# A two-layer graph attention kernel: another order of work in its last stage

## The chip, the cores and the metric

The kernel runs on one core of a Trainium2 chip. The core has five engines that work through their own lists of instructions and wait for each other through semaphores: TensorE (PE, matrix products and transposes), VectorE (DVE, elementwise work and reductions), ScalarE (ACT, functions such as exp), GpSimd (POOL, here the issuer of the gathers) and SyncE (SP, here the issuer of plain transfers). Sixteen DMA engines move data between the large memory (HBM) and the core's own memory (SBUF). TensorE writes its products to a small memory, PSUM, from which VectorE and ScalarE read them.

The metric is the time of one execution on the device in microseconds (us). Before the change the median of three runs is 2330.81 us (2325.15 to 2334.34).

## What is computed

There are 4096 nodes with 512 features each and an adjacency matrix of 4096 by 4096, which is sparse (about 0.2% of its entries are set, many more for the first nodes than for the last). Layer 0 is a graph attention of eight heads; layer 1 is a graph attention of eight heads, a second attention of one head, and a small dense network. Both layers end with a residual sum and a normalisation. What the last stage of the kernel computes is the second half of layer 1:

```python
h2 = _gat_heads(x1, mask, Wo[None], ao[None])[0]     # one head, 512 wide
out = jax.nn.elu(h2)
out = jax.nn.relu(out @ lin1_w + lin1_b)             # 512 -> 1024
return out @ lin2_w + lin2_b                         # 1024 -> 512
...
x = _layernorm(x + _L1_gnn_ref(...), axis=-1)
```

Everything is in 32-bit floats.

## The kernel before, in words

Nodes are taken in 32 tiles of 128. The program first finds the edges of every tile (to about 500 us of the span), then runs the two attentions of eight heads, and then the last stage, from about 1400 us to the end at 2136 us. Only the last stage is changed. A dense path follows for inputs with too many edges, which is not taken with these inputs.

**Units.** The edges of a tile are held in chunks of 128. A unit (`Unit`) is up to six chunks of one tile; small tiles have one or two units, the first tile (the hub) many. For each unit the stage does this:

- `gather` (L1076): GpSimd issues an indirect DMA for each chunk. It fetches the 128 source rows of 514 floats from the table into a buffer `g`. There are four such buffers (`GT`), and a unit's gather is asked for four units ahead, when the sums of the unit that held the buffer have been issued.
- `spread` (L1101 to L1129), once for a tile, two tiles ahead: TensorE spreads the tile's own attention scores over its edges into `pss`; VectorE collects them later (`spread()`), into `s` and `ls`.
- `weights` (L1147 to L1158): three small VectorE steps give `z` from `s`, `ls` and the gathered scores, and ScalarE takes exp of it, giving `w`. It is called one unit ahead.
- `add` (L1187 and L1212): VectorE makes a selection matrix `sm` for each slot (a chunk and one half of the tile), weighted with `w`; TensorE multiplies the gathered rows with it and sums in `acc`. These are the *sums*.

When a tile's sums are complete: `inverse` (L1224) takes the reciprocal of the summed weights, `normal` (L1239) scales the sums to `o`, and `elu` (L1247 to L1249) takes two ScalarE steps to `ex` and returns a last VectorE step that makes the ELU in `o`. `turn` (L1456, L1457) lets TensorE transpose `o` (four transposes to `pt`) and ScalarE copy it to `sht`. There it waits until the tiles of a block (mostly four) are together.

**Pieces.** The dense network runs over blocks. Once the last tile of a block is turned, `ready` receives its pieces: as many of `first_dense` (each two of eight hidden groups, L1479, with bias and relu on ScalarE in L1482) as the block has tiles, and one of `second_dense` for each tile (L1491). A `second_dense` also loads the tile's residual row block `xr` (from `sx_d`, L1487, three buffers), adds the bias (L1488) and leaves a closing part in `open_`: adding the product (L1496), the normalisation on VectorE and ScalarE (L1253 to L1266) and the store (L1498). `close` carries that out; `piece` closes what is open and starts the next piece.

**What sets the order.** The schedule is written out by hand (`manual_schedule`): every engine gets its instructions in the order of the program's calls. A block's pieces are spread over the chunks of the next block: each chunk adds `pace` to `due`, and while `due` is at least 1 a piece is taken. In each step of the loop, before the change, the calls were: scores of a later tile, the turn of a tile that was finished in the step before, weights of the next unit, reciprocal for the tile just ended, this unit's sums, the gather, `close`, `normal` and the whole ELU (`fold`), collection of scores, and at the end the due pieces. After the loop come the last two turns and what is left of the pieces. PSUM holds two buffers for the products of the pieces (`p`), two for `acc`, one each for `pt` and `pss`; `sht` has two buffers and the hidden layer `shid` one.

Of the kernel before, what the change touches and what calls it, by code (L numbers as in the profile page):

```python
# [10 lines left out]
F32 = mybir.dt.float32  # L11
# [10 lines left out]
P = 128  # L22
N = 4096
F = 512
# [534 lines left out]
def sparse_path(  # L559
# [23 lines left out]
    nc = tc.nc  # L583
# [57 lines left out]
    x1_d = dram.tile([N, F], F32, name="sx1_d")  # L641
# [407 lines left out]
    def units_of(order):  # L1049
        units = []  # L1050
        for t in order:
            own = [
                Unit(t, [(p.first + i, n) for i, n in runs], slots)
                for p in pts if p.t == t for runs, *slots in p.units()
            ]
            own[0].first = own[-1].last = True
            units += own
        return units
# [186 lines left out]
    def elu(sb, o):  # L1245
        ex = sb.tile([P, F], F32, name="ex")
        nc.scalar.activation(ex, o, AF.Relu, scale=-1.0)  # L1247
        nc.scalar.activation(ex, ex, AF.Exp, scale=-1.0)  # L1248
        return lambda: nc.vector.scalar_tensor_tensor(o, ex, -1.0, o, op0=OP.add, op1=OP.max)  # L1249

    def layernorm(sb, y):
        bs = sb.tile([P, 6], F32, name="bs")
        nc.vector.bn_stats(bs, y)  # L1253
        mv = sb.tile([P, 2], F32, name="mv")
        nc.vector.bn_aggr(mv, bs)
        rs = sb.tile([P, 2], F32, name="rstd")
        lg, r = rs[:, 0:1], rs[:, 1:2]
        nc.scalar.activation(lg, mv[:, 1:2], AF.Ln, bias=eps)
        nc.scalar.activation(r, lg, AF.Exp, scale=-0.5)

        def rest():

            nc.vector.scalar_tensor_tensor(lg, mv[:, 1:2], EPS, r, op0=OP.add, op1=OP.mult)
            nc.vector.scalar_tensor_tensor(lg, lg, -0.5, r, op0=OP.mult, op1=OP.mult)
            nc.vector.scalar_tensor_tensor(r, lg, 1.5, r, op0=OP.add, op1=OP.mult)
            nc.vector.tensor_scalar(y, y, mv[:, 0:1], r, op0=OP.subtract, op1=OP.mult)  # L1266

        return rest
# [91 lines left out]
    with ExitStack() as pools:  # L1360
        big = pools.enter_context(tc.tile_pool(name="eb", bufs=1))
        sb = pools.enter_context(tc.tile_pool(name="es", bufs=2))
# [24 lines left out]
    sb = ctx.enter_context(tc.tile_pool(name="ls", bufs=2, reuse_waits="tile"))  # L1387
# [23 lines left out]
    with tc.tile_pool(name="tg", bufs=GT, side="right", reuse_waits="tile") as gp, \  # L1411
            tc.tile_pool(name="tb", bufs=1, side="right", reuse_waits="tile") as big, \
            tc.tile_pool(name="ta", bufs=2, space=PSUM, reuse_waits="tile") as pacc, \
            tc.tile_pool(name="tp", bufs=1, space=PSUM, reuse_waits="tile") as ps, tc.manual_schedule():

        few = NT - 12
        blocks = [[NT - 1, NT - 2], [NT - 3 - i for i in range(NJ)]]
        blocks += [[1 + b, few // 2 - b, few // 2 + 1 + b, few - b] for b in range(few // NJ)]  # L1420
        blocks.insert(3, [NT - 9, 0, NT - 8, NT - 7])
        blocks.append([NT - 10, NT - 11])
        assert sorted(sum(blocks, [])) == list(range(NT))
        order = [t for block in blocks for t in block]
        units = units_of(order)
        at = Attention(st2, gp, wk, pacc, ps)
        for _ in range(GT):
            nc.gpsimd.memset(gp.tile([P, GC, F + HS], F32, name="g"), 0.0)
        for u in units[:GT]:
            at.gather(u)  # L1430
        l1w = big.tile([P, FC, HID], F32, name="sl1w")
        nc.sync.dma_start(l1w, lin1_w.rearrange("(c p) o -> p c o", p=P))
        l2w = big.tile([P, HC, F], F32, name="sl2w")
        nc.sync.dma_start(l2w, lin2_w.rearrange("(c p) o -> p c o", p=P))
        l1b_r = big.tile([HC, P], F32, name="sl1b_r")
        nc.sync.dma_start(l1b_r, lin1_b.rearrange("(c p) -> c p", p=P))
        l2b = big.tile([P, F], F32, name="sl2b")
        nc.sync.dma_start(l2b, lin2_b.partition_broadcast(P))
        hts, hids, ready, open_ = {}, {}, [], []

        def fold(t):
            o = at.normal(sb, t)
            elu(sb, o)()
            return o

        def turn(t, o):
            b = next(b for b, block in enumerate(blocks) if t in block)
            j, nb = blocks[b].index(t), len(blocks[b])
            if j == 0:

                while any(r[1] == b - 2 and r[0] is first_dense for r in ready):
                    piece()
                hts[b] = big.tile([P, FC, NB], F32, name="sht", bufs=2)
            pt = ps.tile([P, FC, P], F32, name="pt")
            for c in range(FC):
                nc.tensor.transpose(pt[:, c, :], o[:, ts(c, P)], ident)  # L1456
            nc.scalar.copy(hts[b][:, :, ts(j, P)], pt)  # L1457
            if j == nb - 1:
                per = HC // nb
                ready.extend((first_dense, b, range(i * per, (i + 1) * per)) for i in range(nb))  # L1460
                ready.extend((second_dense, b, i) for i in range(nb))

        def piece():
            close()
            of, *what = ready.pop(0)
            of(*what)

        def close():
            while open_:
                open_.pop(0)()  # L1470

        def first_dense(b, ks):
            if 0 in ks:
                hids[b] = big.tile([P, HC, NB], F32, name="shid")
            for k in ks:
                n = len(blocks[b]) * P
                p1 = ps.tile([P, NB], F32, name="p1", tag="p", bufs=2)[:, :n]
                for c in range(FC):
                    nc.tensor.matmul(  # L1479
                        p1, l1w[:, c, ts(k, P)], hts[b][:, c, :n], start=(c == 0), stop=(c == FC - 1)  # L1480
                    )
                nc.scalar.activation(hids[b][:, k, :n], p1, AF.Relu, bias=l1b[:, k : k + 1])  # L1482

        def second_dense(b, j):
            t = blocks[b][j]
            xr = sb.tile([P, F], F32, name="xr", bufs=3)
            nc.sync.dma_start(xr, x1_d[ts(t, P), :])  # L1487
            nc.vector.tensor_add(xr, xr, l2b)  # L1488
            p2 = ps.tile([P, F], F32, name="p2", tag="p", bufs=2)
            for k in range(HC):  # L1490
                nc.tensor.matmul(  # L1491
                    p2, hids[b][:, k, ts(j, P)], l2w[:, k, :], start=(k == 0), stop=(k == HC - 1)
                )

            def rest():
                nc.vector.tensor_add(xr, p2, xr)  # L1496
                layernorm(sb, xr)()
                nc.sync.dma_start(out[ts(t, P), :], xr)  # L1498

            open_.append(rest)  # L1500

        for t in order[:2]:
            at.spread(t)()
        at.weights(units[0])
        l1b = big.tile([P, HC], F32, name="sl1b")
        pb = ps.tile([P, HC], F32, name="pt")
        nc.tensor.transpose(pb, l1b_r, ident[:HC, :HC])
        nc.vector.tensor_copy(l1b, pb)


        pace = {t: 0.0 for t in blocks[0]}
        for last, block in zip(blocks, blocks[1:]):
            chunks = sum(u.n for u in units if u.t in block)
            pace.update((t, 2 * len(last) / chunks) for t in block)
        due, folded = 0.0, None
        for i, u in enumerate(units):
            pos = order.index(u.t)
            spread = at.spread(order[pos + 2]) if u.first and pos + 2 < NT else None
            if folded:
                turn(*folded)  # L1520
                folded = None
            if i + 1 < len(units):
                at.weights(units[i + 1])
            if u.first and pos > 0:
                at.inverse(sb, order[pos - 1])
            at.add(u)
            if i + GT < len(units):
                at.gather(units[i + GT])
            close()
            if u.first and pos > 0:  # L1530
                folded = order[pos - 1], fold(order[pos - 1])
            if spread:
                spread()
            due = min(due + u.n * pace[u.t], 2.5)
            while due >= 1 and ready:
                due -= 1
                piece()
        if folded:
            turn(*folded)
        at.inverse(sb, order[-1])  # L1540
        turn(order[-1], fold(order[-1]))
        while ready:
            piece()
        close()
# [56 lines left out]
```

## Time and profile before

| What | Value |
|---|---|
| Median of the runs | 2330.81 us |
| The profiled execution, its own time | 2138.83 us |
| Its span, first to last instruction | 2136.3 us |
| TensorE busy, matrix products | 1721.8 us (81%) |
| VectorE, ScalarE, GpSimd busy | 1328.6, 663.4, 1162.0 us |
| Mean granted TensorE clock | 0.918 |
| First dense layer, L1479 | 228.9 us, 576 records |
| Second dense layer, L1491 | 226.7 us, 512 records |
| Sums of the last stage (L1212) from 1400 us on | 200.2 us, 1356 records |

The profile is of one execution, and all durations come from it. A 32-bit matrix product shows as two records. Start times of TensorE's records are measured while their ends are modelled, so a stretch that counts as busy can hold some waiting. "A <- B" in a list of waits means that A stood idle until B had finished. The clock is a share of TensorE's full speed.

### The profile page before, as it was taken

The page shows a single profiled execution, that of the slowest core. Times are in us where ns is not written, and L with a number is a line of the kernel's source. Part 1 is how long each engine was busy: PE and PEld are TensorE (multiplying, and loading weights), DVE is VectorE, ACT ScalarE, POOL GpSimd, SP SyncE. Part 2 cuts the span into 40 slices and gives each one's busy share as a digit, 9 for nine tenths or more (in the row PEclk, how much of TensorE's full clock was granted, in tenths as well). Part 3 has the DMA queues.
Part 4 walks back from the last instruction along what each step waited for, and adds up shares of the span by engine and source line. Part 5 has one row for each costly group of instructions (what it writes and reads, how often), then busy time and mean ns, then how long its engine had stood idle before and what let it go on. Part 6 is the DMA issues. An engine that isn't in the chain of part 4 may idle for free.

```text
span 2136.3 us, 29277 instructions
## 1 busy us (share of the span) xinstructions
PE 1721.8 (81%) x8987; PEld 1004.8 (47%) x8987; DVE 1328.6 (62%) x3920; ACT 663.4 (31%) x2311; POOL 1162.0 (54%) x1662
## 2 busy tenths in 40 slices
PE   4878777663798888857887888569999998998997
PEld 3655443221465565534555655344444444444444
DVE  5787777774889998837878878433434343433413
ACT  3346777664222232102333332111110212111121
POOL 5514444346777777727777777473547443543200
PEclk8999998786999999878999999889999999999999
DMA  6434566544777878727767776463546343534301
GB/s 229 132 109 168 188 250 238 201 153 130 228 233 231 248 242 243 208 67 191 196 185 195 195 198 190 151 165 102 156 119 177 113 128 96 148 103 120 96 19 46
DMA packets 132589, 351.94 MB, mean 165 GB/s; under 512 B 41922, under 2 KB 42954, under 8 KB 128454
## 3 DMA queue, kind: packets, MB, share of 16 engines
q0 software_dynamic: 74160, 206.25, 35.4%
q1 hardware_dynamic: 58262, 143.72, 19.1%
q8 instruction: 74, 1.21, 0.2%
q14 instruction: 93, 0.76, 0.1%
HBM read 347.31 MB, written 42.24 MB: 182 GB/s over the span
## 4 chain that ended last, share of the span: by engine, by line
PE 33%; DVE 17%; issue 16%; POOL 15%; DMA 12%; ACT 6%; SPq 0%; POOLq 0%; DVEq 0%; ACTq 0%
POOL g L1076 10%; DMA g<-table_t,idx 10%; PE acc L1212 10%; PE p L1479 9%; PE ph L697 6%; DVE g L1200 4%; PE p L1491 4%; DVE cand L884 2%; POOL s L944 1%; ACT sides L943 1%; DMA xr<-sx_d 1%; DVE cand L901 1%; DVE sm L1179 1%; DVE lst L899 1%; PE pl L967 1%
## 5 line engine op out<-in xcount | busy, mean ns | idle before, releaser
L1076 POOL DMA_INDIRECT g<-table_t,idx x927 | 937.8, 1012 | 535.9 <-issue 229.1
L1212 PE MATMUL acc<-g,sm 128*64 128x260 f32 (+2 forms) x4068 | 581.0, 416 | 182.7 <-DVE g L1200 141.6
L1212 PEld LDWEIGHTS acc<-g,sm 128*64 128x64 f32 x4068 | 327.9, 148 | 402.1 <-DVE g L1200 159.5
L697 PE MATMUL ph<-sw_t,xt 128*128 128x264 f32 (+1 forms) x1536 | 399.5, 409 | 54.3 <-ACT xt L686 47.8
L697 PEld LDWEIGHTS ph<-sw_t,xt 128*128 128x128 f32 x1536 | 296.5, 199 | 126.3 <-ACT xt L686 70.6
L1200 DVE TENSOR_TENSOR g<-g,wp 128x2048 f32<-128x2048 f32 (+3 forms) x132 | 348.9, 2644 | 3.4 <-ACT wp L1155 3.4
L884 DVE MAX8 cand<-key 128x8 f32<-128x353 f32 (+55 forms) x467 | 196.3, 446 | 77.6 <-PE key L878 76.8
L1479 PE MATMUL p<-sht,sl1w 128*128 128x512 f32 (+1 forms) x576 | 228.9, 553 | 0.5 <-DVE xr L1496 0.5
L1491 PE MATMUL p<-sl2w,shid 128*128 128x512 f32 x512 | 226.7, 597 | 0.0
L686 ACT ACTIVATE xt<-pt 128x128 f32<-128x128 f32 x384 | 101.1, 278 | 214.3 <-PE pt L683 213.9
L1479 PEld LDWEIGHTS p<-sht,sl1w 128*128 128x128 f32 x576 | 108.0, 191 | 111.6 <-issue 106.0
L1491 PEld LDWEIGHTS p<-sl2w,shid 128*128 128x128 f32 x512 | 95.2, 190 | 119.8 <-issue 119.4
L1147 DVE TENSOR_TENSOR z<-s,g 128x16 f32<-128x16 f32 (+8 forms) x291 | 46.6, 175 | 162.7 <-DMA g<-table_t,idx 161.6
L877 PE MATMUL key<-sg,s_identb 128*128 128x512 bf16 (+1 forms) x258 | 111.5, 433 | 14.3 <-DVE cand L884 9.0
L1482 ACT ACTIVATE shid<-p,sl1b 128x512 f32<-128x512 f32 (+1 forms) x72 | 46.0, 639 | 242.8 <-PE p L1479 242.8
L1249 DVE SCALAR_TENSOR_TENSOR o<-ex,o 128x512 f32<-128x512 f32 x64 | 44.2, 691 | 122.0 <-ACT ex L1248 121.8
L848 ACT ACTIVATE sg<-raw 128x4096 bf16<-128x4096 int32 (+1 forms) x39 | 116.9, 2998 | 6.3 <-DMA raw<-in_adj_dram 3.4
L710 ACT COPY hrow<-ph 128x260 f32<-128x260 f32 (+2 forms) x194 | 70.5, 372 | 152.3 <-PE ph L697 152.0
L878 PE MATMUL key<-frac,places 128*128 128x512 bf16 (+1 forms) x258 | 111.4, 433 | 2.7 <-POOL places L784 2.7
L1187 DVE TENSOR_SCALAR sm<-iota_n,nl,w 128x64 f32<-128x64 f32 x339 | 83.6, 327 | 31.2 <-ACT w L1158 31.2
L1155 ACT ACTIVATE wp<-z 128x32 f32<-128x32 f32 (+3 forms) x132 | 27.2, 206 | 211.2 <-DVE g L1200 211.2
L1496 DVE TENSOR_TENSOR xr<-p,xr 128x512 f32<-128x512 f32 x32 | 22.0, 689 | 93.6 <-PE p L1491 93.2
(185 smaller groups left out, 1853.5 us busy)
## 6 DMA issues: line engine op xcount, KB each, us to landing
raw<-in_adj_dram SPq DMA_DIRECT2D x31, 2048.0 KB, 7.7
table_t<-hrow SPq DMA_DIRECT2D x64, 260.0 KB, 3.2
xr<-in_x_dram SPq DMA_DIRECT2D x64, 256.0 KB, 3.9
g<-table_t,idx POOLq DMA_INDIRECT x927, 3.8
table_t<-hrow SPq DMA_DIRECT2D x32, 257.0 KB, 4.4
sx_d<-o SPq DMA_DIRECT2D x32, 256.0 KB, 4.0
xr<-sx_d SPq DMA_DIRECT2D x32, 256.0 KB, 4.4
out_dram<-xr SPq DMA_DIRECT2D x32, 256.0 KB, 2.3
```

The lines of the kernel that those rows point to most:

```text
L686: nc.scalar.activation(xt[:, c, :], pt[:, c, :], AF.Copy, accum_out=st.xparts[:, c, t : t + 1])
L697: nc.tensor.matmul(ph[:n], columns(c), st.w[:, c, j], start=(c == 0), stop=(c == FC - 1))
L848: nc.scalar.activation(sg[:, ts(i, w)], raw[:, ts(i, w)], AF.Sign)
L877: nc.tensor.matmul(out_, ident_b, sg[:, j:e], start=True, stop=False)
L878: nc.tensor.matmul(out_, places[:, w], frac[:, j - w * KW : e - w * KW], start=False, stop=True)
L884: nc.vector.max(out=cand[:, at : at + 8], in_=part)
L1076: nc.gpsimd.indirect_dma_start(out=u.g[:, k, : self.st.row], out_offset=None, in_=self.st.table[:, :], in_offset=bass.IndirectOffsetOnAxis ...
L1187: nc.vector.tensor_scalar(sm[:, at + i], of_g, node[k], u.w[:, k], op0=OP.is_equal, op1=OP.mult)
L1200: nc.vector.tensor_mul(body, body, wp[:, :, :, None].to_broadcast(body.shape))
L1212: nc.tensor.matmul(out_[g * HN : (g + 1) * HN], sm[:, slot], rows(k), start=start, stop=stop)
L1479: nc.tensor.matmul(p1, l1w[:, c, ts(k, P)], hts[b][:, c, :n], start=(c == 0), stop=(c == FC - 1))
L1491: nc.tensor.matmul(p2, hids[b][:, k, ts(j, P)], l2w[:, k, :], start=(k == 0), stop=(k == HC - 1))
```

## The change

It reorders the calls of the last stage's loop, and takes the load of the residual rows out of `second_dense`. In each step the calls now are: scores of a later tile, one due piece if there is one, this unit's sums, the gather, collection of scores, then for a tile that has just ended the reciprocal, `normal` and the two ScalarE steps of the ELU, then the weights of the next unit, the last VectorE step of the ELU, `close`, the turn of a tile finished in an earlier step, and further due pieces. So on ScalarE the exp of the weights stands behind the ELU's two steps, and the turn's copy behind the exp. `due` is added to at the start of a step and no longer at its end. `piece` also loads the residual rows of the next piece if that is a `second_dense`.

```diff
-        hts, hids, ready, open_ = {}, {}, [], []
-
-        def fold(t):
-            o = at.normal(sb, t)
-            elu(sb, o)()
-            return o
+        hts, hids, resid, ready, open_ = {}, {}, {}, [], []
...
             of, *what = ready.pop(0)
+
+            if ready and ready[0][0] is second_dense:
+                rows_of(*ready[0][1:])
             of(*what)
+
+        def rows_of(b, j):
+            t = blocks[b][j]
+            if t not in resid:
+                resid[t] = sb.tile([P, F], F32, name="xr", bufs=3)
+                nc.sync.dma_start(resid[t], x1_d[ts(t, P), :])
...
-            xr = sb.tile([P, F], F32, name="xr", bufs=3)
-            nc.sync.dma_start(xr, x1_d[ts(t, P), :])
+            rows_of(b, j)
+            xr = resid.pop(t)
...
-        due, folded = 0.0, None
+        due, folded = 0.0, []
         for i, u in enumerate(units):
             pos = order.index(u.t)
             spread = at.spread(order[pos + 2]) if u.first and pos + 2 < NT else None
-            if folded:
-                turn(*folded)
-                folded = None
-            if i + 1 < len(units):
-                at.weights(units[i + 1])
-            if u.first and pos > 0:
-                at.inverse(sb, order[pos - 1])
+            due = min(due + u.n * pace[u.t], 2.5)
+            if due >= 1 and ready:
+                due -= 1
+                piece()
             at.add(u)
             if i + GT < len(units):
                 at.gather(units[i + GT])
-            close()
-            if u.first and pos > 0:
-                folded = order[pos - 1], fold(order[pos - 1])
             if spread:
                 spread()
-            due = min(due + u.n * pace[u.t], 2.5)
+            last, rest = units[i - 1].t if u.first and i else None, None
+            if last is not None:
+                at.inverse(sb, last)
+                o = at.normal(sb, last)
+                rest = elu(sb, o)
+            if i + 1 < len(units):
+                at.weights(units[i + 1])
+            if rest:
+                rest()
+            close()
+            if folded:
+                turn(*folded.pop(0))
+            if rest:
+                folded.append((last, o))
             while due >= 1 and ready:
                 due -= 1
                 piece()
-        if folded:
-            turn(*folded)
-        at.inverse(sb, order[-1])
-        turn(order[-1], fold(order[-1]))
+        last = order[-1]
+        at.inverse(sb, last)
+        o = at.normal(sb, last)
+        elu(sb, o)()
+        for what in folded + [(last, o)]:
+            turn(*what)
```

## The prediction

> **What bounds the kernel now.** I read the granted clock first, then the page, the windows by time, the waits of the last stage, and last the timeline around one long wait. The page says TensorE (PE) is the busiest engine, and the change touches the last stage alone. That stage starts about 1400 us into the span and gives PE nearly all the work of the last 690 us.
>
> ```profile
> PE   4878777663798888857887888569999998998997
> PEclk8999998786999999878999999889999999999999
> ```
>
> Row one is PE's busy share in tenths, row two its granted clock. From slice 28 on PE stands at 8 to 9 tenths. A gain can only come from the idle tenth or from the slow clock. I therefore cut the stage where the blocks of dense work begin (the first `first_dense` matmul of each block).
>
> ```profile
> core 0: us, PE busy (x), PEclk, DMA share, GB/s
> 1449.61:1478.30 28.69, 23.56 (x97) 0.94 0.36 109
> 1478.30:1570.48 92.18, 88.73 (x402) 0.96 0.44 125
> 1570.48:1682.35 111.87, 105.26 (x460) 0.97 0.55 158
> 1682.35:1776.98 94.63, 83.84 (x326) 0.93 0.39 114
> 1776.98:1863.64 86.66, 81.36 (x335) 0.98 0.40 115
> 1863.64:1953.54 89.90, 83.78 (x350) 0.98 0.45 128
> 1953.54:2036.03 82.49, 79.89 (x333) 1.00 0.28 84
> 2036.03:2125.25 89.22, 85.94 (x233) 0.98 0.10 30
> ```
>
> Columns: stretch, its length, PE's busy time (count), clock, DMA. Busy time hides some loss, because a matmul that waits inside a group or runs at a low clock counts as busy. So I price PE's work by undisturbed groups of the timeline: a piece (8 wide products, 16 records) takes 6.97 us from start to start, sums 2.75 us for 24 records, a turn 0.55, a score group about 0.2. Length minus work, per row: 8.1, 9.9, 19.5, 17.3, 8.8, 10.7, 4.6, 4.3. **Lost in all: 83 us.**
>
> ```profile
> PE pt L1456 <- DVE o L1249: 29.1, 8, 4.3
> PE acc L1212 <- DVE sm L1187: 12.0, 14, 2.3
> DVE xr L1488 <- DMA xr<-sx_d: 68.3, 21, 5.5
> DVE z L1147 <- DMA g<-table_t,idx: 23.6, 11, 3.6
> ```
>
> These are waits in us, times, longest. Turns wait for the ELU's last step 8 times; sums wait for their selection matrices `sm` 14 times. VectorE (DVE) itself waits 68 us for the residual rows, which are loaded only when needed.
>
> ```profile
> 1845.88 7.13 PE L1491 MATMUL p<-sl2w,shid 128*128 128x512 f32 x16
> 1853.06 1.96 PE L1212 MATMUL acc<-g,sm 128*64 128x257 f32 x16
> 1859.27 1.11 PE L1456 MATMUL pt<-s_ident,o 128*128 128x128 f32 x4 [4.26 <-DVE o L1249]
> 1860.40 3.31 PE L1212 MATMUL acc<-g,sm 128*64 128x257 f32 x16
> 1863.64 7.13 PE L1479 MATMUL p<-sht,sl1w 128*128 128x512 f32 x16
> ```
>
> One block boundary. The piece at 1845.88 is the block's last, so for a while PE has only sums and turns. It idles 4.26 us; then the turn takes 1.11 instead of 0.60 and the sums 3.31 instead of 1.96.
>
> **What the Trainium skill says.** "TensorE: Matmul & The Clock Gate", Part 1, has the array fall to half rate after an idle window of about 3.4 us and recover after as much work. The trace agrees: after gaps of 3.65 to 4.26 us turns last about 1.1 us, while after gaps of 2.60 and 2.73 they last 0.66. So a gap kept under 3.4 us saves a further 1.5 to 3 us. The same page, Part 1 under engine queue depths, calls ScalarE (ACT) and VectorE strict first-in first-out. The trace agrees: at 2051.11 an ELU whose input was ready at 2037.1 starts only after the last bias-and-relu of a piece. Hence program order is what must be followed here. "DMA: Bandwidth & Descriptors" (Anatomy of one DMA) fits a transfer from GpSimd's queue as 2.0 us plus its bytes at 436 GB/s, by estimate 2.6 us for a gather of 128 rows of 514 floats; the trace has 3.7 us from issue to landing, and that is used.
>
> **The change, part by part.** Write S and F for a piece of the second and first dense layer, A for a unit's sums, T for a turn, | for a tile's scores. Instruction counts are unchanged on PE, DVE, ACT, and so are POOL's gathers in number and order; only places change. TensorE's program order over the sixth row's cycle:
> before: F A F | A F T A F | A S T A S | A S T A S | A T A F F
> after: F F A | F A F A T | S A S A T | S A S A T | A A T F F
>
> 1. *Turn one unit later, behind that unit's sums.* Its input is then an ELU from the step before, done while PE summed. The 29.1 us go, except 2.7 at 2053.20 (below), and with them the half clock.
> 2. *Due piece ahead of the sums.* 7 us of PE work cover a unit's `sm`, so the sm waits in the steady part go: 1.0 to 1.4 us each at 1535.9, 1765.1, 1843.6, 1930.2, 1941.1, plus about 0.4 inside each.
> 3. *Residual rows loaded one piece ahead.* SP's queue then has the next load ahead of the previous store (two loads, then store and load in turn), so a load no longer waits for a normalisation. Three buffers hold: one normalised, one used, one landing. DVE's 68 us disappear; PE gains what part 2 counts, plus the tail.
> 4. *Weights before the ELU's last step on DVE, but ACT's exp for them behind the ELU's two ACTIVATEs; the copy behind both.* This costs. Per first unit w comes 1.3 us later (2 x 0.63). Queued behind the ELU's last step on DVE are the normalisation and the next unit's sm, for which PE waits where no piece is due. Also T and F are now adjacent where a block begins: PE waits for the copy, 0.58 plus hand-overs, about 0.9 us.
>
> *Worked boundary, after:* S ends at 0. DVE's closing chain (add 0.69, statistics 0.7 + 0.2, ACT's two 0.5, three of 0.16, scaling 0.55, as at 1853.06 to 1856.5) ends at 3.5. PE: A to 1.9, T to 2.5, scores to 2.75; the next A waits for its first sm at 3.85 (1.1 lost) and ends at 5.9. DVE: sm to 4.6, scores 5.0, reciprocal 0.17, normal 0.74 to 5.9; ACT: ELU 7.2, w 7.4; DVE: last ELU step 7.95, sm 8.3. The third A waits 2.4 us and ends at 10.3, T at 10.9, F starts at 11.9. Lost: 1.1 + 2.4 + 0.9, with edges 4.75 us. No gap reaches 3.4 us. With 12-matmul sums (24 records in place of 16) the waits shrink and it loses 3 to 3.7.
>
> *The sum*, lost after against before by row: 3 for 8.1; 8 for 9.9 (the hub tile's scores in four cuts, 1539 to 1549, stay); 9 for 19.5 (6 is the hub's gather limit: POOL issues a chunk each 1.30 us there without a break); 6.5 for 17.3; 4.75 for 8.8; 4 for 10.7; 4 for 4.6; 2 for 4.3. The last: the wait at 2053.20 stays, since the final ELU is still behind the relus. But the load at 2122.25 no longer holds the last addition (2126.79, though its matmuls ended at 2125.3: 1.5 us), and about 0.8 goes at 2099. Saved: 83 - 41 = 42 us. From this I take off 5, an estimate for gathers: four units' buffers, four to six chunks of 1.30 us plus 3.7 us landing each, are waited for 23.6 us on DVE now under cover, and a quicker PE uncovers some. **37 us.** The profiled execution (2138.83 us) would then take 2102. The runs' median, 2330.81, is 192 us longer, and no view shows where; I carry the difference over unscaled, for a gap made of DVE and ACT latencies has no reason to shrink there: **2294 us**.
>
> Unknown costs: the copy's wait, 0 (the piece's weights already loaded) to 2.5 us (behind a late w), nine times, 0 to 22 us, taken 8. The uncovered gathers, 0 to 15 us, taken 5. The half clock, if the 1.1 and 2.4 us gaps fall in one window, 0 to 2 us at seven boundaries, taken 0.
>
> **Rivals.** *B, the wait only moves:* sums at a boundary wait for the ELU chain as turns did. For it: a third A and both queues in order. Against: the worked chain. At 8 instead of 4.75 us at seven boundaries, 23 us are given back, 14 remain: 2317. *C, slower:* the copy is last in ACT's step, behind w, and w's z waits for a gather. Where a block begins, F needs that copy, so a late gather now stops PE for 7 us (a gather wait as the longest, 3.6, the copy 0.9, and then half clock, 2.5) at eight block starts: 56 - 42 = +14, 2345. It decides from 5.3 us per block start. For it: gathers land barely in time near the hub. Against: at a boundary the needed gather was issued two sums and a piece earlier, some 13 us, and takes 9 to 12. *D, no change:* the runs' extra 192 us are slower gathers, and the stage is bound by them, not by PE's order: 2331. For it: the unexplained difference. Against: nothing in the profile.
>
> **How the numbers follow.** Forecast 0.66 (own range 2272 to 2312), B 0.12, C 0.14, D 0.08. 0.5% is 11.7 us, about what a measurement of this kernel can tell. Faster: 0.66 and half of B, 0.72; same: half of B and D, 0.14; slower: C, 0.14. The range, 2268 to 2326, takes the unknown costs at their ends and B.
>
> **What would show it.** Right: PE's waits on `o` nearly gone, DVE's wait on `xr` near zero, turns of 0.6 us, the clock 1.0 in the 0.93 rows, new waits of sums on `sm` of 1 to 2.4 us at boundaries, about seven. Wrong: gaps above 3.4 us before the first F of a block, or gather waits on DVE above 40 us; then C or B. If the profiled time falls by 37 and the median doesn't, D.

## The result, and the profile after

| | median, us | runs |
|---|---|---|
| before | 2334.49 (2321.84 to 2350.53) | 20 |
| after | 2333.68 (2322.99 to 2344.67) | 20 |

The ratio is 1.0004, with a 95% interval of 0.9987 to 1.0021: no difference, where 37 us less were forecast.

One thing has to be known to read the numbers: the time went with the chip. On one chip the kernel before took 2133 to 2139 us in all its runs, on three others 2321 to 2353 us. They are called the *2135 chip* and the *2335 chips* below. The profile of before shown above has the time of the first sort. The runs to be predicted, and the profile of after, have that of the second.

First the page of after: PE's busy share and clock, and the head of the chain that ended last.

```profile
PE   4777776645676787764667787856979998989998
PEclk9889997766878899886888899877989999999999
PE 52%; DVE 14%; issue 11%; another core or an unknown queue 8%; ACT 6%; POOL 6%; DMA 2%; SPq 0%; POOLq 0%; DVEq 0%; ACTq 0%
```

8% of the chain is put down to a releaser that the profile doesn't know. The page of before has no such entry. The waits of the last stage of after (us, times, longest; "remote" is again the unknown releaser):

```profile
DVE s L1117 <- remote: 36.8, 5, 13.4
ACT sht L1452 <- remote: 17.6, 3, 5.9
PE acc L1212 <- DVE sm L1187: 13.1, 13, 3.6
PE pss L1101 <- DVE s L1117: 10.6, 3, 5.6
PE p L1483 <- ACT sht L1452: 10.4, 4, 4.7
DVE xr L1492 <- DMA xr<-sx_d: 3.2, 1, 3.2
PE pt L1451 <- DVE o L1249: 2.3, 1, 2.3
```

What the change aimed at has happened: the turns' wait for the ELU fell from 29.1 to 2.3 us, VectorE's wait for the residual rows from 68.3 to 3.2. In their place stand waits of the first dense layer for the turn's copy (L1452) and of the scores for their collection (L1117), and both consumers wait for something "remote". Here is such a block start in the timeline (start, length, engine, line, operation, count, idle time before and its releaser):

```profile
1959.44 0.21 ACT L1158 ACTIVATE w<-z 128x6 f32<-128x6 f32 x1 [2.04 <-DVE z L1147]
...
1960.52 1.00 POOL L1076 DMA_INDIRECT g<-table_t,idx  x1 [0.30 <-issue]
...
1960.84 0.66 PE L1451 MATMUL pt<-s_ident,o 128*128 128x128 f32 x4
...
1961.82 1.00 POOL L1076 DMA_INDIRECT g<-table_t,idx  x1 [0.30 <-issue]
...
1963.12 0.99 POOL L1076 DMA_INDIRECT g<-table_t,idx  x1 [0.30 <-issue]
1965.55 0.58 ACT L1452 COPY sht<-pt 128x512 f32<-128x512 f32 x1 [5.90 <-remote]
1965.73 1.00 POOL L1076 DMA_INDIRECT g<-table_t,idx  x1 [1.62 <-remote]
...
1966.19 3.78 PE L1483 MATMUL p<-sht,sl1w 128*128 128x512 f32 x4 [4.70 <-ACT sht L1452]
```

The transposes end at 1961.50. ScalarE has been free since 1959.65. Yet the copy starts at 1965.55, 4.05 us late, while GpSimd issues a gather each 1.30 us; GpSimd then also waits 1.62 us for the unknown. TensorE has nothing else to do and stands for 4.70 us. Afterwards its wide products run 0.85 us apart in place of 0.43. The Trainium skill ("TensorE: Matmul & The Clock Gate", Part 1) has the array at half rate after an idle window of about 3.4 us; the trace agrees here as it did before.

The same happens at two other block starts (3.71 us late at 1871.44, 4.27 at 2050.93) and in the hub tile's scores (1725.4 to 1731.1, where PE waits 5.63, 2.49 and 2.46 us for a collection). At the other four block starts of this stretch the copy is 0.04 to 0.33 us late. Gathers go on around three of these too, but there GpSimd had issued only one, three or four of them since its last pause when the transposes ended; ahead of the three late copies it had issued at least five without a pause. That is a pattern of seven starts and no tested rule.

To compare kernels I use the **dense part**: from the first full-width record of `first_dense` to the end of the last `second_dense`, the prediction's rows two to eight. It is 647.0 us in the profile of before and 652.5 in that of after.

### The profile page after: what moved, and what is told of

The parts are those of the page before. It is cut to its first block, busy times and chain, and to the rows that moved or that the text cites. A ratio compares the mean times of both kernels' runs of the same rounds, so it can differ in the third digit from the quotient of the medians.

```text
span 2320.7 us, 29242 instructions
## 1 busy us (share of the span) xinstructions
PE 1752.6 (76%) x8987; PEld 1020.7 (44%) x8987; DVE 1332.4 (57%) x3920; ACT 661.1 (28%) x2311; POOL 1165.3 (50%) x1662
## 4 chain that ended last, share of the span: by engine, by line
PE 52%; DVE 14%; issue 11%; another core or an unknown queue 8%; ACT 6%; POOL 6%; DMA 2%; SPq 0%; POOLq 0%; DVEq 0%; ACTq 0%
PE acc L1212 15%; PE ph L697 13%; PE p L1483 10%; PE p L1495 9%; DVE g L1200 3%; DVE cand L884 2%; POOL g L1076 2%; PE pt L683 1%; POOL s L944 1%; ACT sides L943 1%; DVE cand L901 1%; DVE lst L899 1%; DMA g<-table_t,idx 1%; PE pl L967 1%
## 5 line engine op out<-in xcount | busy, mean ns | idle before, releaser
L1212 PE MATMUL acc<-g,sm 128*64 128x260 f32 (+2 forms) x4068 | 565.1, 403 | 192.4 <-DVE g L1200 90.3
L697 PE MATMUL ph<-sw_t,xt 128*128 128x264 f32 (+1 forms) x1536 | 432.1, 434 | 139.1 <-ACT xt L686 96.3
L1212 PEld LDWEIGHTS acc<-g,sm 128*64 128x64 f32 x4068 | 316.7, 142 | 426.6 <-issue 147.1
L697 PEld LDWEIGHTS ph<-sw_t,xt 128*128 128x128 f32 x1536 | 319.5, 215 | 220.3 <-ACT xt L686 114.9
L1117 DVE TENSOR_REDUCE s<-pss 128x64 f32<-128x192 f32 (+20 forms) x108 | 32.3, 299 | 123.4 <-remote 80.6
```

The lines of the kernel that those rows point to most:

```text
L697: nc.tensor.matmul(ph[:n], columns(c), st.w[:, c, j], start=(c == 0), stop=(c == FC - 1))
L1212: nc.tensor.matmul(out_[g * HN : (g + 1) * HN], sm[:, slot], rows(k), start=start, stop=stop)
```

## The experiments

The theory at the start was that the moves did save what was worked out, and that something not in the profile of before takes it back. Its rivals were that the reordering never saved anything, or that a part of it costs (weights behind the ELU, copy behind the weights).

**Both kernels again, unedited.**

> The kernel before, unchanged, profiled once more, to compare like with like. 'Dense part' means the time from the first 512-wide product of the first dense layer to the end of the last product of the second: 647.0 us in the first profile of before (1478.3 to 2125.3), 652.5 us in the profile of after (1658.8 to 2311.3). Theory 1 (the profiled execution was a rare one): a normal execution has a span near 2330, in which waits for TensorE's results end 2 to 7 us after the matmul, most of them in the two attention stages; the dense part of before is then longer than 647, about 655 to 690 us, and the change gains little or nothing because its own order is hit as much. Theory 2 (the reasons of the prediction were wrong in themselves): the dense part of before is 645 to 650 us also in a normal execution, and the reordering simply moved its waits.

> The kernel after, unchanged, profiled once more. If its execution is of the short kind (span near 2100 to 2140), theory 1 expects a dense part of about 605 to 620 us, as the prediction worked it out (647 less 37), and theory 2 expects 645 to 652. If it is of the long kind (span near 2320), both expect about 652, with copies to sht that start 3 to 5 us after their transposes at three or more block starts.

On one 2335 chip (before there: 2333.38) they took 2332.8 and 2326.86 us, and their dense parts were 649.0 and 655.0. The dense part of before starts at 1670.29 there and at 1478.30 in its first profile: the 192 us lie ahead of it, and it is itself only 2 us longer. Most of the waits for "remote" that before has on this chip (whole program) lie in that stretch, and the first profile has none anywhere:

```profile
ACT xt L686 <- remote: 123.0, 14, 17.2
ACT hrow L710 <- remote: 82.6, 22, 7.7
POOL g L1076 <- remote: 44.4, 23, 4.0
```

After, run again, has four late copies (2.63 to 5.65 us, one of them just ahead of the dense part), and at the hub's scores TensorE waits 4.25, 3.87 and 2.47 us for collections. So the late results are no accident of one execution.

**Parts of the change, on 2335 chips.** Early load alone, in the kernel before:

```diff
             close()
             of, *what = ready.pop(0)
+            if ready and ready[0][0] is second_dense:
+                rows_of(*ready[0][1:])
...
-            xr = sb.tile([P, F], F32, name="xr", bufs=3)
-            nc.sync.dma_start(xr, x1_d[ts(t, P), :])
+            rows_of(b, j)
+            xr = resid.pop(t)
```

> The kernel before with only the load of the residual rows one piece ahead. The prediction put the waits behind late residual rows at about 5 x 1.5 us in the steady part and 2.3 us at the end: theory 1 and the prediction expect 5 to 12 us less than before (0.2 to 0.5%), theory 2 expects no difference (within 3 us).

The kernel after with the turn ahead of the sums, so that sums lie between a turn and the first dense layer:

```diff
+            if folded:
+                turn(*folded.pop(0))
             at.add(u)
...
             close()
-            if folded:
-                turn(*folded.pop(0))
```

> The kernel after with one edit: the turn of an older tile is issued ahead of the unit's sums in place of behind them, so that where a block's first piece starts, a unit's sums lie between the transposes and the matmuls that need their copy. Theory 1 (late copies at block starts are what gave the gain back: 4.4, 4.7 and 4.9 us of waiting at three starts, each followed by some 2 us at half clock) expects 15 to 30 us less than after. Theory 2 (the waits move to wherever the chain on VectorE ends) expects within 5 us of after.

That order again with the next unit's `weights` called ahead of `inverse`, `normal` and the ELU:

> As the version with the turn ahead of the sums, and with the next unit's weights ahead of the reciprocal, the norm and the ELU of the tile just ended, so that their exp stands ahead of the ELU's two steps on ScalarE. By the worked boundary the next sm is 1.3 us (two ELU steps) earlier at some nine places without a due piece: 5 to 12 us less than the version it is made from, if the chain over ScalarE bounds there; no difference (within 4 us) if late signals from TensorE do. A gather that is late now holds the norm as well, which could cost up to 5 us.

The kernel after without the early load (the three lines in `piece` taken out):

> The kernel after without the early load of the residual rows: the reordering alone. The early load alone made before 20.8 us faster. If the two parts add up, this is 15 to 25 us slower than before (ratio 1.006 to 1.011); if the reordering only took away what the early load could still give (both fill the same holes), it is within 5 us of before.

| kernel | us | runs | ratio to before, 95% interval | dense part |
|---|---|---|---|---|
| early load alone | 2312.6 | 6 | 0.9904 (0.9874 to 0.9933) | 639.8 |
| turn ahead of the sums | 2318.02 | 7 | 0.9931 (0.9900 to 0.9963) | 637.7 |
| and weights first | 2335.91 (before there 2344.59) | 22 | 0.9960 (0.9948 to 0.9973) | 645.9 |
| after without early load | 2374.47 (before there 2344.59) | 5 | 1.0138 (1.0114 to 1.0162) | 670.5 |

On these chips the early load is worth 1% alone, and the other moves of the change cost what it brings. It saved more than the 5 to 12 us expected; the profiled execution, the slowest of the six, has 9.2 us in its dense part, and the rest wasn't traced. Where the sums lie behind the turn, TensorE goes on working, and the copy has only to be done by their end: in the dense part one copy is 2.41 us late, no wide product waits for a copy, and the part is 17 us shorter than that of after on the same chip. Putting the weights first doesn't help further. The reordering without the early load cost 30 us, more than the 15 to 25 expected.

**Is it the gathers?** In the last stage of both kernels the gather is replaced by plain loads of as many rows of the table on SyncE's queue. These fetch wrong rows, so the gather is left out; all other work stays.

```diff
             for k, c in enumerate(u.chunks):
+                if self.st.heads == 1:
+                    nc.sync.dma_start(u.g[:, k, : self.st.row], self.st.table[ts(c % NT, P), :])
+                    continue
                 nc.gpsimd.indirect_dma_start(
```

> The kernel before, whose last stage loads each chunk with a plain DMA of 128 table rows from SyncE in place of GpSimd's indirect gather: the bytes move, GpSimd issues nothing, the rows are not the right ones. Theory G (while GpSimd issues gathers back to back, a result of TensorE that nothing follows on TensorE is signalled only when that run of issues ends): before has few such results in its dense part, so it stays near 649 us less the hub's gather limit, 632 to 645. Theory P (a result is late whenever TensorE pauses, whoever else works): no change beyond the hub, the same 632 to 645.

> The kernel after with the same plain loads. Theory G: the copies to sht start within 0.3 us of their transposes at all block starts (3.7 to 4.3 us late at three of them in after), the collections of the hub's scores likewise (2.3 to 5.4 us late), and the dense part is 605 to 622 us, against 652 to 655 with gathers: at least 15 us below the plain version of before. Theory P: the copies stay 3 to 6 us late at three or more block starts and the dense part is within 8 us of the plain version of before.

Each ran once. Before became slower (2369.69 against 2344.59), missed its forecast and tells nothing of gathers: its residual loads now stand behind the plain loads on SyncE, and VectorE waits 184.5 us for them. After fell to 2291.61 us on the same chip, and its dense part to 619.0. Its waits have no "remote" left in the last stage, and the first dense layer waits 0.7 us at most for a copy:

```profile
PE p L1486 <- ACT sht L1455: 5.4, 8, 0.7
PE pt L1454 <- DVE o L1252: 2.3, 1, 2.3
PE pss L1104 <- DVE s L1120: 1.2, 4, 0.3
```

So with no gathers from GpSimd the late results are gone from the change's order. (How much the order itself saves can't be read from this, because the plain version of before gives no base.) What it is about a gather was left: its issue, a GpSimd that is merely busy, or the wait for the rows. Two more kernels load as the last one does and give GpSimd something useless to do for each load, either a gather into a buffer that nothing reads, or a fill of about the same length (0.84 us against 1.00):

```diff
                     nc.sync.dma_start(u.g[:, k, : self.st.row], self.st.table[ts(c % NT, P), :])
+                    spare = self.gp.tile([P, P], F32, name="spare", bufs=4)
+                    nc.gpsimd.indirect_dma_start(
+                        out=spare,
+                        out_offset=None,
+                        in_=x1_d.rearrange("n (q w) -> (n q) w", w=P),
+                        in_offset=bass.IndirectOffsetOnAxis(ap=idx[:, c : c + 1], axis=0),
...
                     continue
```

```diff
                     nc.sync.dma_start(u.g[:, k, : self.st.row], self.st.table[ts(c % NT, P), :])
+                    spare = self.gp.tile([P, 896], F32, name="spare", bufs=1)
+                    nc.gpsimd.memset(spare, 0.0)
                     continue
```

> The plain-load version of after, and beside each plain load GpSimd issues one indirect gather of 128 rows of 512 bytes into a spare buffer that nobody reads (the output is that of the plain version). These gathers wait for nothing but their own buffers, so GpSimd issues all 309 back to back, some 400 us of issuing, until about 1980 to 2050 of the span, and is silent afterwards. Theory G (back-to-back issuing of gathers on GpSimd holds back TensorE's signals) expects copies to sht 2 us or more late at most block starts while the issuing lasts, none after it, and a dense part 15 us or more above the 619.0 us of the plain version. Theory D (a late signal needs GpSimd itself to wait for TensorE, or the gathered rows to be used) expects copies within 0.3 us throughout and a dense part of 617 to 625.

> The same with a memset of 128 x 896 floats on GpSimd in place of each idle gather (0.78 us each by the 2.70 us that 3120 columns take), so GpSimd is as busy but issues no DMA. If it is the issuing of DMAs that matters, copies stay within 0.3 us and the dense part at 617 to 625; if any busy GpSimd holds signals back, copies are late as with gathers in the first half of the stage and the dense part is 630 or more.

These ran on the 2135 chip (before there 2135.2): 2106.93 and 2112.56 us, no late copy in either. A second pair ran there too, with 2108.41 and 2107.81 us and dense parts of 618.3 and 620.7:

> The changed kernel with the last stage's gathers replaced by plain loads of as many rows from SyncE's queue (wrong rows, so the output is not the reference's), and GpSimd issuing as many gathers into a buffer that nothing reads. On a chip where the kernel before takes 2330 us or more: if GpSimd's issue of gathers makes TensorE's signal late, three or more copies begin over 2 us after their transposes' end and the dense part is 640 to 660 us; if it is the wait for the gathered rows or their use, no copy is over 0.5 us late and the dense part is 615 to 630 us. On a chip where the kernel before takes 2135 us: no late copy, about 618 us, and nothing is told apart.

> As the run with idle gathers, but GpSimd fills a tile (memset) in place of each gather: it is busy and issues no DMA. If a busy GpSimd is enough to make TensorE's signal late, three or more copies begin over 2 us late and the dense part is 640 to 660 us on a chip where the kernel before takes 2330 us or more; if it takes the issue of gathers, no copy is over 0.5 us late and the dense part is 615 to 630 us.

They show that the same issues at the same 1.30 us do no harm on that chip. The third pair ran on a 2335 chip (before there 2337.11):

> The idle gathers once more (the last stage's rows by plain loads, wrong rows; GpSimd issues as many gathers into a buffer that nothing reads), in the hope of a chip where the kernel before takes 2330 us or more. There: if GpSimd's issue of gathers makes TensorE's signal late, three or more copies begin over 2 us late and the dense part is 640 to 660 us; if it is the wait for the gathered rows or their use, no copy is over 0.5 us late and the dense part is 615 to 630 us. Where the kernel before takes 2135 us: about 2107 us, no late copy, nothing told apart.

> The memsets once more (as the idle gathers, GpSimd fills a tile in place of each gather), in the hope of a chip where the kernel before takes 2330 us or more. There: if a busy GpSimd is enough, three or more copies begin over 2 us late and the dense part is 640 to 660 us; if it takes the issue of gathers, no copy is over 0.5 us late and the dense part is 615 to 630 us. Where the kernel before takes 2135 us: about 2110 us, no late copy.

With the fills it took 2285.02 us; with the idle gathers **2651.85 us** (one execution each). Nothing reads what they fetch, so GpSimd is hardly held back, and it issues 309 gathers from 1559 to 1970 us nearly without a break. The waits of that stretch in the run with idle gathers:

```profile
DVE s L1129 <- remote: 332.4, 4, 201.1
ACT sht L1464 <- remote: 152.2, 2, 76.4
ACT shid L1498 <- remote: 150.8, 5, 63.9
```

and one of its block starts:

```profile
1805.78 1.00 POOL L1079 DMA_INDIRECT spare<-sx_d,idx  x1 [0.30 <-issue]
1807.08 1.00 POOL L1079 DMA_INDIRECT spare<-sx_d,idx  x1 [0.30 <-issue]
1807.53 0.58 ACT L1464 COPY sht<-pt 128x512 f32<-128x512 f32 x1 [76.44 <-remote]
...
1808.17 0.80 PE L1495 MATMUL p<-sht,sl1w 128*128 128x256 f32 x1 [88.48 <-issue]
```

The transposes had ended at 1719.69 and ScalarE was free from 1731.09; the copy came 76.4 us later. Both engines, VectorE at the scores and ScalarE at the copy and the relu, wait for results of TensorE. The last late one is at 1993.05, 23 us after the last issue, and from then on every copy at a block start is 0.04 us late. The dense part starts only at 2026.5, behind all gathers, and takes 614.1 us. So the loss lies ahead of it, and two copies are late, where three and a dense part of 640 to 660 us were expected.

TensorE itself is slow there too:

```profile
1701.82 0.59 PE L1224 MATMUL acc<-g,sm 128*64 128x256 f32 x1 [2.21 <-issue]
1704.62 0.59 PE L1224 MATMUL acc<-g,sm 128*64 128x256 f32 x1 [2.21 <-issue]
1707.43 0.58 PE L1224 MATMUL acc<-g,sm 128*64 128x256 f32 x1 [2.22 <-issue]
```

These are the last three of 24 records of sums that begin between 1644.42 and 1707.43, mostly 2.80 us apart. Elsewhere 24 such records take 2.75 us in all, and at half clock 5.89 us (at 1584.97 in this run). Most of them wait for no semaphore, and VectorE had finished its last `sm` at 1644.15. The hand-overs between the other engines stay prompt: VectorE's `o` ended at 1640.77 and ScalarE began on it 0.03 us later. So what is slow under the gathers is TensorE, in its results and also in its own next instructions.

In the run with fills, a block start while GpSimd is just as busy looks like this:

```profile
1742.17 3.58 POOL L1079 MEMSET spare<- 128x896 f32 x4
...
1743.16 0.66 PE L1456 MATMUL pt<-s_ident,o 128*128 128x128 f32 x4
...
1743.86 0.59 ACT L1457 COPY sht<-pt 128x512 f32<-128x512 f32 x1 [0.87 <-PE pt L1456]
...
1744.49 0.70 PE L1488 MATMUL p<-sht,sl1w 128*128 128x512 f32 x1 [0.68 <-ACT sht L1457]
```

It is 0.04 us from the transposes' end to the copy, and the dense part is 621.6 us long. So the cause lies in the gathers of GpSimd themselves, not in a busy GpSimd and not in a wait for their rows, which nothing reads. Bytes alone are an unlikely cause: an idle gather moves 66 KB, and the plain loads move 263 KB each by SyncE in the run without late results too.

**The change on the 2135 chip.** If this is all, the change must bring its gain where no result is late. The kernel after, unedited:

> The changed kernel again, nothing edited, timed in five rounds. Theory (late signals of TensorE at block starts eat the gain, and they come only on chips that also have the 192 us of late results): if the kernel before takes about 2135 us on this chip, the changed one saves 20 to 40 us, its dense part is 605 to 625 us long and no turn's copy begins more than 0.5 us after the transposes' end; if the kernel before takes 2330 to 2345 us, the ratio is 0.995 to 1.003, the dense part 650 to 656 us, and three or four copies begin 2.5 to 6 us late. Rival (the gain was never there: the reordering alone costs as much as the early load saves, on any chip): ratio 0.998 to 1.002 and a dense part above 640 us on either kind of chip.

2105.32 us against 2135.01: ratio **0.9853 (0.9827 to 0.9880)**, five runs. Here are its dense part and that of after on the 2335 chip, cut at the block starts (stretch, length, PE busy and count, clock, DMA share, GB/s). First the 2335 chip:

```profile
1658.81:1759.85 101.04, 87.19 (x401) 0.93 0.40 117
1759.85:1875.79 115.94, 105.24 (x457) 0.97 0.54 150
1875.79:1966.19 90.40, 82.62 (x325) 0.95 0.41 119
1966.19:2055.84 89.65, 81.90 (x334) 0.98 0.37 108
2055.84:2142.39 86.55, 83.51 (x348) 0.98 0.46 128
2142.39:2225.16 82.77, 80.03 (x332) 1.00 0.32 92
2225.16:2311.32 86.16, 83.81 (x232) 1.00 0.08 28
```

Then the same kernel on the 2135 chip:

```profile
1475.28:1566.11 90.83, 86.99 (x401) 0.98 0.45 129
1566.11:1673.32 107.21, 103.41 (x457) 0.98 0.56 158
1673.32:1756.69 83.37, 79.62 (x325) 1.00 0.43 126
1756.69:1839.92 83.23, 79.72 (x334) 1.00 0.40 120
1839.92:1924.61 84.69, 81.81 (x348) 1.00 0.48 137
1924.61:2007.36 82.75, 80.03 (x331) 1.00 0.31 92
2007.36:2093.52 86.16, 83.81 (x232) 1.00 0.08 28
```

The last two stretches, with few gathers left, agree to 0.02 us. The first five differ by 10.2, 8.7, 7.0, 6.4 and 1.9 us, in sum 34.3: that is where the gain goes.

The first holds the hub's scores. Late copies end the second, third and fourth. The fifth has none; behind the last late copy the clock is at half for 3.4 us, which by estimate (half of that) is worth 1.7 of its 1.9 us. 5 of the second's 8.7 us lie ahead of its late copy and weren't traced further. One copy on the 2135 chip is late, just ahead of the dense part: by 3.04 us, behind a `w` whose `z` had waited 4.20 us for a gather. That is the case which the prediction priced at up to 2.5 us, and it occurs once.

A block start on the 2135 chip, with the same gathers around it:

```profile
1838.59 0.66 PE L1451 MATMUL pt<-s_ident,o 128*128 128x128 f32 x4
1838.59 1.00 POOL L1076 DMA_INDIRECT g<-table_t,idx  x1 [0.30 <-issue]
...
1839.28 0.59 ACT L1452 COPY sht<-pt 128x512 f32<-128x512 f32 x1 [1.64 <-PE pt L1451]
...
1839.89 1.00 POOL L1076 DMA_INDIRECT g<-table_t,idx  x1 [0.30 <-issue]
...
1839.92 1.12 PE L1483 MATMUL p<-sht,sl1w 128*128 128x512 f32 x2 [0.68 <-ACT sht L1452]
```

**Versions on the 2135 chip.** The first text belongs to the early load alone. The other two belong to one kernel with one move more, the ELU ahead of the closing part of the piece (in the kernel before); the turn that the last text speaks of was not moved:

```diff
-            close()
             if u.first and pos > 0:
                 folded = order[pos - 1], fold(order[pos - 1])
+            close()
```

> The early load alone once more, beside the version above on the same chip: ratio 0.987 to 0.993 to before, as measured first (0.9904).

> The version of before with the early load, and with the norm and the ELU of the tile just ended ahead of the closing part of the piece on VectorE. At a block's end the ELU no longer stands behind the 3.5 us of closing work, so the waits of turns on o (4.26 us at three block ends, 2.6 to 3.3 us at three more, each of the long ones with some 2 us at half clock behind it) should go, at the price of some 1.5 us of sums waiting for sm. Turns still lie ahead of sums, so no signal is waited for with TensorE idle. Expected: 12 to 28 us less than the early load alone, that is a ratio of 0.979 to 0.986 to before. If late signals take this up too, no difference from the early load alone (within 5 us).

> The kernel before with the residual tile loaded a step early and one older tile's turn put ahead of the sums' order as in the earlier run of this kernel. That run took 2101.68 us where the kernel before took 2135.2 (ratio 0.984). If its gain does not depend on the late signals, the ratio is 0.980 to 0.990 on either kind of chip; if late signals at block starts eat it as they do the changed kernel's, the ratio is 0.990 to 1.000 on a chip where the kernel before takes 2330 us or more.

The early load alone took 2122.96 us (0.9937, 0.9925 to 0.9949, six runs); with the ELU first it was 2101.68 (0.9839, 0.9826 to 0.9851, five runs) and, run again, 2104.07 (0.9855, 0.9839 to 0.9872, four runs), the same as the kernel after there, so this version doesn't separate from it. It wasn't tried on a 2335 chip. There the early load alone (0.9904) and the turn ahead of the sums (0.9931) are the best against before, and their intervals overlap.

## Why the prediction was wrong

**The step that failed** is the copy's wait, which the prediction listed as an unknown cost of "0 (the piece's weights already loaded) to 2.5 us (behind a late w)", together with "I carry the difference over unscaled". The copy did not wait behind a late `w`: `w` had been done for 1.6 to 2.2 us when the transposes ended. It waited for TensorE's result itself, 3.7 to 4.3 us at three block starts, which is enough to bring the half clock as well (3.4 to 6.8 us of it, by estimate 1.7 to 3 us more); the stretch with the hub's scores lost 10. No view of the profile of before could show this, for there no result was late. But the profile's own time was 192 us below the median of the runs, and that difference was not a constant to be added. The stretch that holds it is full of the same late results, and a new order can expose more of them. (That they make up all of the 192 us isn't shown: no run took the gathers out of the earlier stages.) Before loses only 2 us of its dense part to them (649.0 us on a 2335 chip, 647.0 in its first profile); its block starts put sums between the turn and the first dense layer. After has 34 us of it (652.5 and 618.2), since there turn, copy and wide product follow directly on each other.

**What held**, and what did not, by its own steps:

- *Part 1.* 2.7 us of the turns' wait were to stay; 2.3 stayed.
- *Part 2.* The waits of sums on `sm` did not shrink but move: 12.0 us before, 13.1 after.
- *Part 3.* VectorE's wait for residual rows was to disappear: 3.2 us are left. Alone, the early load saves 21 us on a 2335 chip (2333.38 to 2312.6) and 12 on the 2135 chip.
- *Part 4, the boundary.* Waits of 1.1, 2.4 and 0.9 us were worked out; the run on the 2135 chip has 1.10, 1.74 to 1.84 and 0.67 at two boundaries; at the others the sums mostly wait less.
- *The sum.* Before in its first profile and after on the 2135 chip differ by 28.7 us over the rows two to eight, where the rows as predicted give 36.9. One row makes most of the difference: the hub's, where 10.5 us were to go and 4.7 went (111.9 to 107.2); the other six were predicted at 26.4 and gave 24.1. The dense part starts 3.0 us sooner and the rest behind it is 1.6 us shorter, so the profiled executions differ by 33.3 us; the measured medians differ by 29.7. The 5 us taken off for gathers bring the sum near this, but not for their reason, so that is luck. The forecast of 2102 us for the profiled execution stands beside 2105.32.

**The rivals.** B: no; the sums' waits at the boundary are those of the forecast. C named the right place, the copy that the first dense layer needs at a block start, and nearly the right size with the half clock, but not the cause (a late gather), and it set in at three of the eight starts. D came nearest in time and did name the gathers, but its reason is wrong: not slower gathers bound the stage, for the dense part of before is nearly as long on both sorts of chip.

The lesson is in the chance given to D: a 9% gap between the profiled execution and the runs was known, unexplained, and given 0.08.

## What to carry to other kernels

When the profiled execution is far from the timed ones, find out where the difference lies before pricing anything: the profile may come from a chip without the cost that decides. A dependent chain through TensorE, ScalarE and back (transpose, copy, product) should have independent TensorE work in it; sums between turn and product were worth 0.7% on the 2335 chips where the direct hand-over gave nothing. The loads that depend on nothing recent could be issued a step early here, and that won on both sorts of chip.

## What the runs showed of the hardware

On three of four chips, results of TensorE reached ScalarE, VectorE and GpSimd late while GpSimd was issuing indirect DMAs back to back: 2.6 to 5.7 us at block starts of the kernel after, 76 us in an unbroken run of 309. In that run TensorE's own instructions came 2.80 us apart too. Fills of the same number did nothing, and nor did plain loads of as many rows from SyncE. On the fourth chip the same programs showed none of it, and the kernel before took 9% less time. The Trainium skill ("DMA: Bandwidth & Descriptors", SWDGE vs HWDGE vs iDMA) says that GpSimd builds its descriptors by software and writes them to rings, and that transfers from SyncE don't use that path; the runs agree in that only GpSimd's DMAs did harm.

What stays open is which part of that path holds up TensorE, why the last late result came 23 us after the last issue, and why one chip is free of it. The ends of TensorE's records are modelled, so whether the work or only its signal is late isn't told apart.

One rival was not tested. In the profiles from the 2335 chips, records of semaphore updates are missing while gathers run: that of after holds 1299 for the 1787 instructions of ScalarE that make such an update, and none is missing in its first 500 us, where GpSimd gathers nothing. The same kernel's profile from the 2135 chip holds all 1787. So the recording is disturbed in the same stretches as TensorE. The timed executions on record have a traced span and clock too; whether TensorE would be late on these chips with nothing recorded isn't known. Missing records also make labels unsure: some waits marked "issue" there, such as the 88.48 us before the product at 1808.17, are waits for a ScalarE copy whose own record is missing.
